# Softmax part between a product and its eviction, weight sums' DMAs on the GpSimd queue, tile pieces in twos, tail products two and then one

## The chip, the cores and the metric

The kernel runs on one core of a Trainium2 chip. The metric is the device time of one execution in microseconds (us). Before the change three runs gave 3805.22, 3813.81 and 3816.59; the median is 3813.81.

## The reference, cut to what matters

Two layers work on `x` of shape (2, 768, 64, 64), float32. Layer 0 is a Mamba block (input projection, 3x3 depthwise convolution, selective scan, layer norm, output projection). Layer 1 is an attention without keys; it and the end of layer 0 are what the change touches. `_gn` is a group norm over 32 groups.

```python
x = x + _L0_conv_ref(_gn(x), ...)
x = x + _L1_conv_ref(_gn(x), W_qkv, W_out, temp)

def _L1_conv_ref(x, W_qkv, W_out, temp):          # 12 heads of 64 channels, N = 4096 tokens
    w = (x3 @ W_qkv.T)                            # product 1, "p1": 768 x 768
    w_normed = w / max(norm over tokens, 1e-12)
    logits = sum over the head's channels of w_normed ** 2, times temp
    Pi = softmax(logits, over the heads)
    dots = sum over tokens of Pi / sum(Pi) * w ** 2
    out = -(w * Pi) / (1 + dots)
    return out @ W_out.T                          # product 3, "p3": 768 x 768
```

## The kernel before

All data are float32. Of each of the two images, layer 1 has 8 column tiles (`j`) of 512 tokens, and 768 channels are 6 chunks (`m` or `k`) of 128. A plain product of one (image, tile, chunk) is six 128x128 by 128x512 matmuls, which the profile counts as twelve instructions.

**Order.** The order of instructions is written by hand (`manual_schedule`); an engine runs its own in that order. What an engine's queue holds behind a waiting instruction waits too, and this is also so for SP, which issues most DMAs. Buffers of 512 columns are 46 slots, 79 from layer 1 on, in one list: `take` pops the oldest, `give` appends. Weights have 4 buffers (`wst`, `N_WEIGHT = 4`).

**Tail of layer 0.** `step(g)` runs one channel chunk through all stages of a pipeline. `scan(g)` (L512, L514) and `times_c(g)` (L521) are on VectorE. `out_proj(g)` (L574) is twelve steps behind and needs, every fourth step, `out_evict` (L586, VectorE) to free its two PSUM banks. When the input projections are used up, `step` does plain p1 products of image 0 in their place, one a step (`pq`, L663), evicted by ScalarE (L673, L674), all in the PSUM bank of `psA`. There are `N_TAIL` = 32 of them.

**Between.** Then `product` (`half_a`, `half_b`; tiles `mm`, L663 or L698) does the rest, with the banks `psA` and `psC` in turn. `half_a` loads weights up to four products ahead. Five products run beside the group norm of image 1, seven beside `weight_sums`, four more follow. `weight_sums` loads four quarter chunks of a weight matrix (L774), adds and subtracts them on GpSimd (L775 to L778) and stores four results to DRAM (`s_dr`, L782); loads and stores are issued by SP, the stores after the next product.

**Attention.** `attention(b)` goes over the 8 tiles: squares on ScalarE (L943), `head_rows` (L960), `head_columns` (L971), `softmax_a` (L977 to L980), `softmax_b` (L986 to L991 on VectorE, the transpose `pt` L995 on TensorE, its copy `pit` L999 on ScalarE), `spread` (L1011), `times_pi` (L1017) and `pi_sums` (L1024) on VectorE. One plain product is put into each tile as filler: its first half between `times_pi` and `softmax_a`, its second half before `softmax_b`. In `attention(0)` the filler is a p1 product, evicted on ScalarE; in `attention(1)` it is a p3 product, evicted on VectorE (L707) and stored by SP (L684).

**Block series.** The other products are done by `strassen`, which takes 7 half-size products for 8: a block is a (tile, `m`) with seven products of three 128x256 matmuls (L852). Series 1 has six p3 tiles of image 0 and six p1 tiles of image 1, series 2 the eight p3 tiles of image 1. Each tile needs twelve sums on GpSimd (`tile_sums`, L807), and before them six ScalarE operations: `scale_v` (L693) for p3, `norm_x1` (L651) for p1. `times` loads block weights up to seven halves ahead (L847). In a block ScalarE copies a product to `p5` (L906), VectorE adds it (L910), and the fifth product of the block waits for that. For p3, GpSimd adds `p5` too (L908). `copy` is L891, `evict` L875, L876 and L879, and the filling operations of the next tile come all at once at the start of a block.

Of the kernel before, what the change touches and what calls it, by code (L numbers as in the profile page):

```python
# [58 lines left out]

N_TAIL = BEHIND + 3 + AHEAD + 2  # L60

# [6 lines left out]
def both_layers(  # L68
# [621 lines left out]

    def scale_v(b, j):
        for k in range(KM):
            nc.scalar.activation(w1s[b, k, j], w1s[b, k, j], AF.Copy, scale=ats[b][:, k : k + 1])  # L693

    def p3_mm(d, w, po, ks):
# [41 lines left out]

    def half_b():
        p = cur["p"]
        kind, d = order[0][p]  # L740
        (p1_mm if kind == "p1" else p3_mm)(d, ready[p][0], cur["ps"], range(3, KM))
        if kind == "p1":
            p1_evict(d, cur["ps"])
            for t in cur["new"]:
                norm_x1(*t)
        else:
            p3_evict(d, cur["ps"], ready[p][1])
        ready[p] = None
# [20 lines left out]
    def weight_sums(kind, m):  # L769
        w = {"p1": qkvP, "p3": woutP}[kind]  # L770
        t = [take() for _ in range(6)]
        a11, a12, a21, a22, s1, s2 = [v[:, : KH * P].rearrange("p (k m) -> p k m", k=KH) for v in t]
        for v, (r, h) in zip((a11, a21, a22, a12), ((m, 0), (m + KH, 0), (m + KH, 1), (m, 1))):
            nc.sync.dma_start(v, w[r][:, h * KH : (h + 1) * KH, :])  # L774
        nc.gpsimd.tensor_add(s1, a21, a22)  # L775
        nc.gpsimd.tensor_sub(s2, s1, a11)
        nc.gpsimd.tensor_sub(a21, a11, a21)
        nc.gpsimd.tensor_sub(a12, a12, s2)  # L778

        def store():  # L780
            for q, v in enumerate((s1, s2, a21, a12)):
                nc.sync.dma_start(s_dr[kind][m, q], v)  # L782
            for v in t:
                give(v)

        return store

# [9 lines left out]
    def tile_sums(kind, b, j):  # L797
        x = [x1s[b, j, k] if kind == "p1" else w1s[b, k, j] for k in range(KM)]
        t = [take() for _ in range(5)]
        halves = [v[:, h] for v in t for h in (lo, hi)]  # L800
        b11, b12 = [[v[:, h] for v in x[:KH]] for h in (lo, hi)]
        b21, b22 = [[v[:, h] for v in x[KH:]] for h in (lo, hi)]
        t1, t3, t4 = [halves[KH * q : KH * (q + 1)] for q in range(3)]
        t2 = b12
        for o, p, q in ((t1, b12, b11), (t3, b22, b12), (t2, b22, t1), (t4, b21, t2)):
            for k in range(KH):
                nc.gpsimd.tensor_sub(o[k], p[k], q[k])  # L807
        tiles[kind, b, j] = {"b11": b11, "b21": b21, "b22": b22, "t1": t1, "t2": t2, "t3": t3, "t4": t4, "held": t}

    def tile_done(kind, b, j):  # L810
# [5 lines left out]

    def tile_prepare(kind, b, j, part):
        if part == 0:
            if kind == "p1":
                for k in range(KM):  # L820
                    load_x1(b, j, k)
            else:
                scale_v(b, j)
        elif kind == "p1" and part == 1:
            for k in range(KM):
                norm_x1(b, j, k)
        elif part == (2 if kind == "p1" else 1):
            tile_sums(kind, b, j)

    def strassen(todo, beside={}):  # L830

# [4 lines left out]
        seq = [v for v in seq if v[0] < len(blocks)]  # L836
        have, xr, at = {}, {}, {"load": 0, "use": 0}

        def times(dst, what, start=False):

            i = at["use"]
            while at["load"] < min(i + 7, len(seq)):
# [6 lines left out]
                at["load"] += 1  # L849
            full, half = have[i]  # L850
            for k in range(KH):
# [41 lines left out]

        load_res(0)
        y = first(0)
        x = copy(0, y)
        for q, (kind, b, j, m) in enumerate(blocks):
            load_res(q + 1)
            at_tile = q // KH
            if at_tile + 1 < len(todo):  # L900
                tile_prepare(*todo[at_tile + 1], q % KH)
            w = bank(psO, "po0", q)
            times(w[:, lo], "t1", start=True)
            times(x[:, lo], "b21")
            p5 = wk.tile([P, TL], F32, tag="sq", name=f"p5_{'_'.join(map(str, blocks[q]))}", bufs=3)[:, lo]
            nc.scalar.copy(p5, w[:, lo])  # L906
            if kind == "p3":
                nc.gpsimd.tensor_add(xr[q, 1][:, hi], p5, xr[q, 1][:, hi])  # L908
            times(y[:, lo], "t2")
            nc.vector.tensor_add(x[:, hi], y[:, lo], p5)  # L910
            y2 = first(q + 1) if q + 1 < len(blocks) else None
            evict(q, x[:, lo], 0, 0)
            times(y[:, lo], "t3")
            if kind == "p1":
                w1s[b, m + KH, j] = take()
                c22 = w1s[b, m + KH, j][:, hi]
                nc.vector.tensor_add(c22, y[:, lo], p5)
                nc.scalar.activation(
                    w[:, lo], c22, AF.Square, accum_out=ss[b][:, m + KH, 2 * j + 1 : 2 * j + 2]
                )  # L920
            else:
                evict(q, y[:, lo], 1, 1)
            times(x[:, hi], "b22")
            times(y[:, lo], "t4")
            if m == KH - 1:
                tile_done(kind, b, j)
            evict(q, x[:, hi], 0, 1)
            if kind == "p3":
                store_out(b, j, m, xr.pop((q, 0)))
            if y2 is not None:  # L930
                x = copy(q + 1, y2)
            evict(q, y[:, lo], 1, 0)
            if kind == "p3":
                store_out(b, j, m + KH, xr.pop((q, 1)))
            y = y2
            if q in beside:
                beside[q]()

# [88 lines left out]
    def attention(b, lead, more, behind):  # L1027
# [11 lines left out]
        for j in range(NQ):  # L1039
# [12 lines left out]
            pi_sums(b, j, range(2))  # L1052
            half_b()
            if not last:
                softmax_b(b, j + 1)
            times_pi(b, j, (4, 5))
# [19 lines left out]
        ats[b] = at  # L1076
        for part in range(3):
            tile_prepare(*behind, part)
        product(more)
# [7 lines left out]
    with tc.manual_schedule():  # L1087
# [23 lines left out]
        for v in range(N_EARLY[1]):  # L1111
            gn_piece(1, v)

        def step(g, prep=None):
            a, n = g + AHEAD, g + AHEAD + 2
# [3 lines left out]
            if n + 1 < NQ0:  # L1119

                for q in (n + 1, n + 2) if g < 0 else (n + 1,):
                    if q not in wis:
                        load_wi(q)
            elif NQ0 <= n + 1 < NQ0 + N_TAIL:
                wis[n + 1] = load_w1(qkvP[(n + 1) % KM])
            if BEHIND <= g + 1 < NQ0 + BEHIND:
# [11 lines left out]
            if n < NQ0:  # L1138
                in_proj(n)
            elif n < NQ0 + N_TAIL:  # L1140
                pas[n] = psA.tile([P, 512], F32, tag="psa", name=f"pq{n}")
                p1_mm(P1[n - NQ0][1], wis.pop(n), pas[n], range(KM))
            if g % 2 == 1 and 0 <= g - 5 < NQ0:
# [32 lines left out]
            if n < NQ0:  # L1176
# [13 lines left out]
            elif n < NQ0 + N_TAIL:  # L1190
                d = P1[n - NQ0][1]
                p1_evict(d, pas.pop(n))
                for k in {2: [0], 3: [1], 4: [2], 5: [3, 4, 5]}.get(d[2], []):
# [133 lines left out]
        for load, pe, dve in gn_next(1):  # L1327
# [3 lines left out]
            dve()  # L1331
        store = lambda: None
        for kind in ("p3", "p1"):
            for m in range(KH):
                product()
                store()
                store = weight_sums(kind, m)
        product()
        store()
        product(n1 - N_TAIL - 6 - 2 * KH)  # L1340
        todo = [("p3", 0, j) for j in range(NQ - N_FILL)] + [("p1", 1, j) for j in range(N_FILL, NQ)]
        attention(0, 1, 1, todo[0])
        beside = {3 * len(todo) - 6 + 2 * q: (lambda j: lambda: scale_v(0, j))(NQ - N_FILL + q) for q in range(N_FILL)}
        strassen(todo, beside)
        todo = [("p3", 1, j) for j in range(NQ)]
        attention(1, 1, 1, todo[0])
        strassen(todo)


# [133 lines left out]
```

## Time and profile before

| | |
|---|---|
| runs | 3805.22, 3813.81, 3816.59 us |
| profiled execution | 3809.74 us, its span 3808.0 us |
| busy in the span | PE 3571.5 (94%), DVE 2842.5 (75%), ACT 2562.5 (67%), POOL 1715.7 (45%) |
| matmul of the plain product | 12 instructions, 5.15 us where nothing holds them |
| matmul of the block product | 6 instructions, 1.29 us; 7 of them in 9.06 us a block |

PE is TensorE, PEld its weight loads, DVE VectorE, ACT ScalarE, POOL GpSimd, SP the queue that issues DMAs. Times in the text count from the start of the span. The stages, read from the timeline: layer 0 alone up to 2518; its last steps with the tail products up to 2886; products with group norm and weight sums up to 2988; `attention(0)` up to 3101; series 1 up to 3445; `attention(1)` up to 3583; series 2 to the end. A row of the timeline has start, duration, engine, line, operation, output<-input, shapes, count, and in brackets the engine's idle time before it with what ended it.

### The profile page before, as it was taken

Reading aid. Unit: us, or ns where it says so; the run is one execution under the profiler, and the core shown is the slowest. Engines: PE = TensorE matmul, PEld = TensorE weight load, DVE = VectorE, ACT = ScalarE, POOL = GpSimd, SP = SyncE. Lnnn points to the kernel's source line nnn. Section 1 sums busy time; section 2 is a strip of 40 time slices with the busy share of each in tenths; the row PEclk is TensorE's granted clock in tenths of the full one; section 3 lists DMA queues with packets and bytes.
Section 4 is the critical chain, followed back from the end, with each engine's and each line's share of the span. In section 5 each row is a group of like instructions: output and inputs, shape, how many; then the busy total and the mean of one; then the engine's idle time right before and its main releaser. Section 6 shows DMA issues by size and latency. Waiting matters only on the chain.

```text
span 3808.0 us, 36991 instructions
## 1 busy us (share of the span) xinstructions
PE 3571.5 (94%) x10882; PEld 1721.9 (45%) x10882; DVE 2842.5 (75%) x2554; ACT 2562.5 (67%) x4940; POOL 1715.7 (45%) x1713
## 2 busy tenths in 40 slices
PE   5877999999999999999999999999999999999899
PEld 3422333333333333333343333333344468884588
DVE  7699999999999999999999999997500342225422
ACT  2588888888888888888888888886523531343211
POOL 0255555565555555555555555654301023220142
PEclk9988999999999999999999999999999999999999
DMA  9677898998988989899898999976645348753487
GB/s 353 181 174 150 183 211 172 207 209 189 211 177 203 208 189 209 179 205 207 182 207 174 208 203 194 205 172 166 156 127 179 123 137 271 234 178 101 129 271 244
DMA packets 374921, 730.80 MB, mean 192 GB/s; under 512 B 43280, under 2 KB 111312, under 8 KB 370624
## 3 DMA queue, kind: packets, MB, share of 16 engines
q0 software_dynamic: 142560, 259.59, 40.8%
q1 hardware_dynamic: 232160, 468.85, 37.0%
q8 instruction: 88, 1.44, 0.2%
q14 instruction: 113, 0.93, 0.1%
HBM read 433.88 MB, written 60.03 MB: 130 GB/s over the span
## 4 chain that ended last, share of the span: by engine, by line
PE 41%; DVE 32%; DMA 8%; ACT 8%; issue 6%; POOL 3%; SPq 0%; DVEq 0%; POOLq 0%; ACTq 0%
DVE s L514 12%; PE po L574 7%; PE pa L352 7%; DVE acc L436 7%; PE po_p L852 6%; DVE s L512 5%; DVE da L521 5%; DMA u<-ysum 4%; PE psa_p L852 4%; PE acc_p L852 4%; PE mmp L663 3%; PE pq L663 3%; PE mmp L698 2%; POOL ysum L501 1%; ACT tm L402 1%
## 5 line engine op out<-in xcount | busy, mean ns | idle before, releaser
L352 PE MATMUL pa<-u,w 128*128 128x512 f32 (+1 forms) x2304 | 1048.7, 606 | 22.6 <-ACT carry L367 15.5
L574 PE MATMUL po<-u,w 128*128 128x512 f32 x2304 | 1036.7, 599 | 26.3 <-DVE u L586 26.3
L514 DVE TENSOR_TENSOR_SCAN s<-da,s 128x2052 f32<-128x2052 f32 x192 | 851.1, 4433 | 19.5 <-ACT u L307 0.5
L352 PEld LDWEIGHTS pa<-u,w 128*128 128x128 f32 x2304 | 434.4, 194 | 622.9 <-issue 492.0
L574 PEld LDWEIGHTS po<-u,w 128*128 128x128 f32 x2304 | 429.3, 190 | 619.2 <-issue 560.0
L501 POOL TENSOR_TENSOR ysum<-da 128x1024 f32<-128x1024 f32 x192 | 384.4, 2002 | 580.7 <-DVE da L521 455.4
L436 DVE SCALAR_TENSOR_TENSOR acc<-xs,pc,acc 128x512 f32<-128x512 f32 x741 | 558.3, 753 | 39.3 <-PE acc L422 12.9
L489 ACT ACTIVATE da<-dl,neg_a 128x512 f32<-128x512 f32 x768 | 489.7, 713 | 0.0
L512 DVE TENSOR_TENSOR s<-du,bc 128x2048 f32<-128x2048 f32 x192 | 438.9, 2286 | 57.8 <-POOL du L493 56.7
L408 POOL DMA_DIRECT2D tm<-tm x309 | 267.2, 865 | 447.0 <-ACT tm L402 408.1
L521 DVE TENSOR_TENSOR da<-s,bc 128x2048 f32<-128x2048 f32 x192 | 440.0, 2292 | 6.3
L508 POOL DMA_DIRECT2D u<-ysum x384 | 377.9, 1246 | 3.4 <-issue 2.4
L390 ACT ACTIVATE acc<-xs,pc 128x512 f32<-128x512 f32 x192 | 132.3, 689 | 282.8 <-DVE u L436 281.6
L402 ACT ACTIVATE tm<-xs,pc 128x512 f32<-128x512 f32 x486 | 317.1, 718 | 3.9 <-DMA tm<-tm 3.2
L493 POOL TENSOR_TENSOR du<-dl,u 128x512 f32<-128x512 f32 x192 | 243.5, 1268 | 0.0
L414 POOL DMA_DIRECT2D u<-tm x177 | 204.2, 1154 | 57.2 <-issue 41.2
L852 PE MATMUL po_p<-u,w 128*128 128x256 f32 x648 | 165.4, 384 | 0.0
L436 DVE SCALAR_TENSOR_TENSOR u<-xs,pc,acc 128x512 f32<-128x512 f32 x192 | 143.6, 748 | 9.5 <-DVE acc L436 0.4
L477 PE MATMUL pz<-xd,dt_w 48*128 48x512 f32 x384 | 113.1, 667 | 35.5 <-DVE gs_x L193 14.9
L505 ACT ACTIVATE u<-u,pc 128x512 f32<-128x512 f32 x192 | 137.0, 714 | 5.3 <-POOL du L493 5.2
L663 PE MATMUL pq<-u,w 128*128 128x512 f32 x300 | 135.2, 596 | 2.2 <-ACT pq L674 1.3
L443 ACT ACTIVATE u<-u,pc 128x512 f32<-128x512 f32 x192 | 124.4, 712 | 16.2 <-DMA u<-tm 15.7
(285 smaller groups left out, 4733.7 us busy)
## 6 DMA issues: line engine op xcount, KB each, us to landing
u<-ysum POOLq DMA_DIRECT2D x384, 256.0 KB, 5.6
tm<-tm POOLq DMA_DIRECT2D x309, 256.0 KB, 4.4
w<-in_wP SPq DMA_DIRECT2D x192, 384.0 KB, 4.6
w<-wo_dr SPq DMA_DIRECT2D x192, 384.0 KB, 4.9
u<-x SPq DMA_DIRECT2D x276, 256.0 KB, 5.2
w<-s_dr_p SPq DMA_DIRECT2D x240, 192.0 KB, 3.7
u<-tm POOLq DMA_DIRECT2D x177, 256.0 KB, 5.9
bc<-bc_dr SPq DMA_DIRECT2D x32, 1024.0 KB, 7.1
```

Of the source, the lines that this page charges most:

```text
L352: nc.tensor.matmul(pa[:, :nn], w[:, k, :], xts[i, k][:, :nn], start=(k == 0), stop=(k == KM - 1))
L402: nc.scalar.activation(tm.rearrange("p (h w) -> p h w", w=W), xs[:, dy : dy + TR, dx : dx + W], AF.Copy, scale=pc[:, c, PC_W + j : PC_W + ...
L436: nc.vector.scalar_tensor_tensor(dst, xs[:, dy : dy + TR, dx : dx + W], pc[:, c, PC_W + j : PC_W + j + 1], acc, ALU.mult, ALU.add)
L489: nc.scalar.activation(das[g % 2][:, n, 1:], deltas[g], AF.Exp, scale=neg_a[:, c, n : n + 1])
L501: nc.gpsimd.tensor_add(ysum[:, 0 : 2 + g % 2 : 1 + g % 2, :], da[:, 0:2, 1:], da[:, 2:4, 1:])
L508: nc.gpsimd.dma_start(us[g], ysums(g, n), accum_op=ALU.add)
L512: nc.vector.tensor_mul(s[:, :, 1:], dus.pop(g).unsqueeze(1).to_broadcast([P, NS, TL]), bc[:, :NS, :])
L514: nc.vector.tensor_tensor_scan(sf, das[g % 2].rearrange("p n l -> p (n l)"), sf, 0.0, ALU.mult, ALU.add)
L521: nc.vector.tensor_mul(das[g % 2][:, :, 1:], s[:, :, 1:], bc[:, NS:, :])
L574: nc.tensor.matmul(po[e], w[:, kk, e * P : (e + 1) * P], us[i * KI + k], start=(k == 0), stop=(k == KI - 1))
L663: nc.tensor.matmul(pa, w[:, k, :], x1s[b, j, k], start=(k == 0), stop=(k == KM - 1))
L852: nc.tensor.matmul(dst, half[:, k, :], tiles[blocks[seq[i][0]][:3]][what][k], start=(start and k == 0), stop=(k == KH - 1), skip_group_che ...
```

## The change

- Tail: 33 products, and step `NQ0 - 1` (the last with a scan) does two of them; from the sixth on, odd ones use the bank of `psC`.
- `weight_sums` issues its loads and stores on GpSimd's queue, stands before the product beside which it was, and stores at once.
- `half_b` takes a function that runs between its matmuls and its eviction; `attention` passes `softmax_b`.
- `strassen` is split: `prepare` (residual loads, the first six half weights, the first tile's scaling and sums) is called in `attention` before its last product; `products` does the rest.
- The ScalarE and GpSimd operations for the next tile are queued as single jobs and issued in twos at three places of a block (GpSimd's in fours in the third block of a tile). The two p3 tiles left for `attention(1)` are scaled in this way in the last tile of series 1.

```diff
-N_TAIL = BEHIND + 3 + AHEAD + 2
+N_TAIL = BEHIND + 3 + AHEAD + 2 + 1
...
-    def half_b():
+    def half_b(between=lambda: None):
...
         (p1_mm if kind == "p1" else p3_mm)(d, ready[p][0], cur["ps"], range(3, KM))
+        between()
         if kind == "p1":
             p1_evict(d, cur["ps"])
...
         for v, (r, h) in zip((a11, a21, a22, a12), ((m, 0), (m + KH, 0), (m + KH, 1), (m, 1))):
-            nc.sync.dma_start(v, w[r][:, h * KH : (h + 1) * KH, :])
+            nc.gpsimd.dma_start(v, w[r][:, h * KH : (h + 1) * KH, :])
...
-        def store():
-            for q, v in enumerate((s1, s2, a21, a12)):
-                nc.sync.dma_start(s_dr[kind][m, q], v)
-            for v in t:
-                give(v)
-        return store
+        for q, v in enumerate((s1, s2, a21, a12)):
+            nc.gpsimd.dma_start(s_dr[kind][m, q], v)
+        for v in t:
+            give(v)
...
+        def prepare():
+            load_res(0)
+            load(6)
+            run(tile_scalar(*todo[0]))
+            run(tile_sums(*todo[0]))
...
+        def jobs_of(q):
+            at_tile, part = divmod(q, KH)
+            if at_tile + 1 == len(todo):
+                if part == 0:
+                    scalar_jobs.extend(last)
+                return
+            kind, b, j = todo[at_tile + 1]
+            if kind == "p1" and part == 0:
+                for k in range(KM):
+                    load_x1(b, j, k)
+            if part == (1 if kind == "p1" else 0):
+                scalar_jobs.extend(tile_scalar(kind, b, j))
+            if part == (2 if kind == "p1" else 1):
+                pool_jobs.extend(tile_sums(kind, b, j))
+
+        def some_jobs(q):
+            run(scalar_jobs, 2)
+            run(pool_jobs, 4 if q % KH == 2 else 2)
...
                 nc.scalar.copy(p5, w[:, lo])
                 if kind == "p3":
                     nc.gpsimd.tensor_add(xr[q, 1][:, hi], p5, xr[q, 1][:, hi])
+                some_jobs(q)
                 times(y[:, lo], "t2")
                 nc.vector.tensor_add(x[:, hi], y[:, lo], p5)
                 y2 = first(q + 1) if q + 1 < len(blocks) else None
                 evict(q, x[:, lo], 0, 0)
+                some_jobs(q)
                 times(y[:, lo], "t3")
...
                 if y2 is not None:
                     x = copy(q + 1, y2)
+                some_jobs(q)
                 evict(q, y[:, lo], 1, 0)
...
-            half_b()
-            if not last:
-                softmax_b(b, j + 1)
+            half_b(lambda: last or softmax_b(b, j + 1))
...
-        for part in range(3):
-            tile_prepare(*behind, part)
+        behind()
         product(more)
...
+        def tail(g):
+            q = g + AHEAD + 2 - NQ0
+            return [v for v in ([q] if g < NQ0 - 1 else [q, q + 1] if g == NQ0 - 1 else [q + 1]) if 0 <= v < N_TAIL]
...
-            elif n < NQ0 + N_TAIL:
-                pas[n] = psA.tile([P, 512], F32, tag="psa", name=f"pq{n}")
-                p1_mm(P1[n - NQ0][1], wis.pop(n), pas[n], range(KM))
+            for q in tail(g):
+                bank, tag = (psC, "acc") if q > 3 and q % 2 else (psA, "psa")
+                pas[NQ0 + q] = bank.tile([P, 512], F32, tag=tag, name=f"pq{q}")
+                p1_mm(P1[q][1], wis.pop(NQ0 + q), pas[NQ0 + q], range(KM))
...
             for m in range(KH):
+                weight_sums(kind, m)
                 product()
-                store()
-                store = weight_sums(kind, m)
-        product()
-        store()
-        product(n1 - N_TAIL - 6 - 2 * KH)
+        product(n1 - N_TAIL - 5 - 2 * KH)
```

More of the change, by code (lines that the diff above doesn't have):

```diff
@@ L689, in p3_load @@
         return load_w1(woutP[d[2]]), xr
-    def scale_v(b, j):
-        for k in range(KM):
-            nc.scalar.activation(w1s[b, k, j], w1s[b, k, j], AF.Copy, scale=ats[b][:, k : k + 1])
     def p3_mm(d, w, po, ks):
@@ L804, in tile_sums @@
         t2 = b12
-        for o, p, q in ((t1, b12, b11), (t3, b22, b12), (t2, b22, t1), (t4, b21, t2)):
-            for k in range(KH):
-                nc.gpsimd.tensor_sub(o[k], p[k], q[k])
+        jobs = [
+            (lambda o, p, q: lambda: nc.gpsimd.tensor_sub(o, p, q))(o[k], p[k], q[k])
+            for o, p, q in ((t1, b12, b11), (t3, b22, b12), (t2, b22, t1), (t4, b21, t2)) for k in range(KH)
+        ]
         tiles[kind, b, j] = {"b11": b11, "b21": b21, "b22": b22, "t1": t1, "t2": t2, "t3": t3, "t4": t4, "held": t}
+        return jobs
     def tile_done(kind, b, j):
@@ L814, in tile_done, with tile_scalar, piece, run @@
             give(t)
-    def tile_prepare(kind, b, j, part):
-        if part == 0:
+    def tile_scalar(kind, b, j):
+        def piece(k):
             if kind == "p1":
-                for k in range(KM):
-                    load_x1(b, j, k)
-            else:
[L823 to L830, printed above, removed]
+                norm_x1(b, j, k)
+            else:
+                nc.scalar.activation(w1s[b, k, j], w1s[b, k, j], AF.Copy, scale=ats[b][:, k : k + 1])
+        return [(lambda k: lambda: piece(k))(k) for k in range(KM)]
+    def run(jobs, n=None):
+        for _ in range(len(jobs) if n is None else min(n, len(jobs))):
+            jobs.pop(0)()
+    def strassen(todo, last=()):
         blocks = [t + (m,) for t in todo for m in range(KH)]
@@ L837, in strassen, with load @@
         have, xr, at = {}, {}, {"load": 0, "use": 0}
-        def times(dst, what, start=False):
-            i = at["use"]
-            while at["load"] < min(i + 7, len(seq)):
+        scalar_jobs, pool_jobs = [], []
+        def load(until):
+            while at["load"] < min(until, len(seq)):
                 q, w = seq[at["load"]]
@@ L849, in times @@
                 at["load"] += 1
+        def times(dst, what, start=False):
+            i = at["use"]
+            load(i + 7)
             full, half = have[i]
@@ L892, in copy @@
             return x
[L894 to L937, printed above, removed]
@@ new lines, in some_jobs, with products @@
+        def some_jobs(q):
+            run(scalar_jobs, 2)
+            run(pool_jobs, 4 if q % KH == 2 else 2)
+        def products():
+            y = first(0)
+            x = copy(0, y)
+            for q, (kind, b, j, m) in enumerate(blocks):
+                load_res(q + 1)
+                jobs_of(q)
+                w = bank(psO, "po0", q)
+                times(w[:, lo], "t1", start=True)
+                times(x[:, lo], "b21")
+                p5 = wk.tile([P, TL], F32, tag="sq", name=f"p5_{'_'.join(map(str, blocks[q]))}", bufs=3)[:, lo]
+                nc.scalar.copy(p5, w[:, lo])
+                if kind == "p3":
+                    nc.gpsimd.tensor_add(xr[q, 1][:, hi], p5, xr[q, 1][:, hi])
+                some_jobs(q)
+                times(y[:, lo], "t2")
+                nc.vector.tensor_add(x[:, hi], y[:, lo], p5)
+                y2 = first(q + 1) if q + 1 < len(blocks) else None
+                evict(q, x[:, lo], 0, 0)
+                some_jobs(q)
+                times(y[:, lo], "t3")
+                if kind == "p1":
+                    w1s[b, m + KH, j] = take()
+                    c22 = w1s[b, m + KH, j][:, hi]
+                    nc.vector.tensor_add(c22, y[:, lo], p5)
+                    nc.scalar.activation(
+                        w[:, lo], c22, AF.Square, accum_out=ss[b][:, m + KH, 2 * j + 1 : 2 * j + 2]
+                    )
+                else:
+                    evict(q, y[:, lo], 1, 1)
+                times(x[:, hi], "b22")
+                times(y[:, lo], "t4")
+                if m == KH - 1:
+                    tile_done(kind, b, j)
+                evict(q, x[:, hi], 0, 1)
+                if kind == "p3":
+                    store_out(b, j, m, xr.pop((q, 0)))
+                if y2 is not None:
+                    x = copy(q + 1, y2)
+                some_jobs(q)
+                evict(q, y[:, lo], 1, 0)
+                if kind == "p3":
+                    store_out(b, j, m + KH, xr.pop((q, 1)))
+                y = y2
+            run(scalar_jobs)
@@ L940, in squares @@
+        return prepare, products
     def squares(b, j):
@@ L1123, in step @@
                         load_wi(q)
-            elif NQ0 <= n + 1 < NQ0 + N_TAIL:
-                wis[n + 1] = load_w1(qkvP[(n + 1) % KM])
+            for q in tail(g + 1)[: int(g != NQ0 - 1)]:
+                wis[NQ0 + q] = load_w1(qkvP[q % KM])
             if BEHIND <= g + 1 < NQ0 + BEHIND:
@@ L1139, in step @@
                 in_proj(n)
-            elif n < NQ0 + N_TAIL:
-                pas[n] = psA.tile([P, 512], F32, tag="psa", name=f"pq{n}")
-                p1_mm(P1[n - NQ0][1], wis.pop(n), pas[n], range(KM))
+            for q in tail(g):
+                bank, tag = (psC, "acc") if q > 3 and q % 2 else (psA, "psa")
+                pas[NQ0 + q] = bank.tile([P, 512], F32, tag=tag, name=f"pq{q}")
+                p1_mm(P1[q][1], wis.pop(NQ0 + q), pas[NQ0 + q], range(KM))
+            for q in tail(g + 1)[int(g != NQ0 - 1) :]:
+                wis[NQ0 + q] = load_w1(qkvP[q % KM])
             if g % 2 == 1 and 0 <= g - 5 < NQ0:
@@ L1189, in step @@
                         norm_x1(0, 0, k)
-            elif n < NQ0 + N_TAIL:
-                d = P1[n - NQ0][1]
-                p1_evict(d, pas.pop(n))
+            for q in tail(g):
+                d = P1[q][1]
+                p1_evict(d, pas.pop(NQ0 + q))
+                if d[1] == (N_TAIL - 1) // KM:
+                    continue
                 for k in {2: [0], 3: [1], 4: [2], 5: [3, 4, 5]}.get(d[2], []):
@@ L1331, in both_layers @@
             dve()
-        store = lambda: None
         for kind in ("p3", "p1"):
             for m in range(KH):
+                weight_sums(kind, m)
                 product()
-                store()
-                store = weight_sums(kind, m)
-        product()
-        store()
-        product(n1 - N_TAIL - 6 - 2 * KH)
[L1341 to L1347, printed above, removed]
+        product(n1 - N_TAIL - 5 - 2 * KH)
+        rest = range(NQ - N_FILL, NQ)
+        scaled = []
+        prepare, products = strassen([("p3", 0, j) for j in range(NQ - N_FILL)] + [("p1", 1, j) for j in range(N_FILL, NQ)], scaled)
+        attention(0, 1, 1, prepare)
+        for j in rest:
+            scaled += tile_scalar("p3", 0, j)
+        products()
+        prepare, products = strassen([("p3", 1, j) for j in range(NQ)])
+        attention(1, 1, 1, prepare)
+        products()
 @with_exitstack
```

## The prediction

> **What bounds the kernel now.** First the page: busy shares and slices.
>
> ```profile
> PE 3571.5 (94%) x10882; PEld 1721.9 (45%) x10882; DVE 2842.5 (75%) x2554; ACT 2562.5 (67%) x4940; POOL 1715.7 (45%) x1713
> PE   5877999999999999999999999999999999999899
> DVE  7699999999999999999999999997500342225422
> ```
>
> Up to slice 27 VectorE and TensorE are both full; from about 2640 us on only TensorE is, and all that the change touches lies there. So an edit is worth what it takes from TensorE's idle time after 2640. The second view is the list of TensorE's waits from 2560 on (who, for whom, us in total, times, longest):
>
> ```profile
> PE pt L995 <- DVE pi L990: 17.1, 9, 3.8
> PE po L574 <- DVE u L586: 9.0, 3, 5.1
> PE acc_p L852 <- DVE po_p L910: 7.5, 6, 4.5
> PE psa_p L852 <- DMA w<-woutP: 7.3, 1, 7.3
> PE mmp L663 <- ACT v L651: 6.0, 1, 6.0
> PE pq L663 <- ACT pq L674: 3.8, 3, 1.3
> PE psa_p L852 <- DVE po_p L910: 1.6, 2, 0.8
> ```
>
> Six places, of which the change addresses each. The third view, the timeline of TensorE, shows what a wait costs beyond itself:
>
> ```profile
> 2740.39 7.88 PE L574 MATMUL po<-u,w 128*128 128x512 f32 x12 [5.09 <-DVE u L586]
> 2952.67 2.07 PE L663 MATMUL mmp<-v,w 128*128 128x512 f32 x2 [6.01 <-ACT v L651]
> 2954.54 3.97 PE L663 MATMUL mmp<-u,w 128*128 128x512 f32 x6
> 2960.92 2.74 PE L663 MATMUL mmp<-u,w 128*128 128x512 f32 x6
> 3486.64 1.16 PE L995 MATMUL pt<-ident,pi 128*128 128x128 f32 x8 [1.65 <-DVE pi L990]
> 3582.92 1.19 PE L852 MATMUL psa_p<-v,w 128*128 128x256 f32 x2 [7.30 <-DMA w<-woutP]
> ```
>
> After idle times over about 3 us matmuls run at half speed for a while (twelve take 7.88 us instead of 5.31; six 3.97 instead of 2.74). I count this with each wait.
>
> **The change part by part**, all times in the profiled execution (3809.7 us).
>
> *Tail 2-1.* At 2740.39 `po` waits for L586, which stands in VectorE's queue behind the last scan (L514 at 2732.97, L521 at 2737.44). That chain takes nothing from the tail products, so the release stays. TensorE ended its tail product at 2735.1; with one product more (5.15 us) it arrives at 2740.25. Idle 5.1 and slow clock 7.88 - 5.31 = 2.6 go: 7.7 us, since the moved product disappears later. Cover: the fourth tile's last x pieces, now wanted at 2735; ScalarE evicts the second product at about 2728.8 to 2730.2 and norms four pieces (2.9 us for four at 2871.94) by about 2733.5. If that is late, up to 5.1 comes back. SP's loads of weights stay within four buffers; each is issued when a product or `out_proj` frees one.
>
> *Two banks in the tail.* The last two of the waits for L674 (1.27 each) go. But the first product after the tail waits for weights (1.85 us), which SP issues behind two stores of sums (L608) that follow the last-but-one eviction on ScalarE. This eviction moves forward by 1.4, not 2.5, relative to the last `out_proj`. Gain 1.4 (0 to 2.5).
>
> *Weight sums on GpSimd's queue.* At 2952.67 TensorE waits for a norm (L651) of a piece that SP loaded only at 2946.60, behind stores waiting for GpSimd's sums:
>
> ```profile
> 2940.85 3.31 SPq L782 DMA_DIRECT2D s_dr_p<-v  x4
> 2946.60 0.43 SPq L648 DMA_DIRECT2D v<-x  x1
> ```
>
> With these on GpSimd, SP never waits for sums. Gone are 6.0, the slow clock 1.05 + 1.23 = 2.3, and 0.7 at 2977.26, where ScalarE was late from another such piece: 9.0. New on GpSimd: 8 DMA issues a set, bounded by its own DMA rows (0.87 at L408 to 1.25 at L508), 4 sums of 0.99, a load's landing between 2.6 (SP's weight quarters) and 5.8 (L594): 13.5 to 20 us a set, I take 15, nearer the plain rows. Queued behind a waiting GpSimd instruction are only the next sets. GpSimd is idle from 2867.6, and the slots that the first sets take were returned many steps before, so six sets run to about 2958. About 33 slots are free in the list at the first set, and set and product take 8; a slot of set k comes round four sets later, when it has been stored. The series read `s_dr` at 3098. Cost 0.
>
> The Trainium skill, "DMA: Bandwidth & Descriptors", section "Issuing engines are not separate DMA queues", speaks against this part: transfers of all issuing engines share the same DMA engines, and another issuer only saves the sequencer's time to issue. By that rule alone this part is worth nothing and the sum is 9.0 smaller. The rows above show more than issue time, namely SP's waiting for GpSimd (L782), which the rule doesn't speak of.
>
> *First weights of a series.* Series 2 begins with 7.3 idle; its weights were issued at 3577.78, behind the store of the last filler product (3576.37), landing 5.0 later. Now they follow the store before, at 3571.00: issue at 3572.4, landing 3577.4, and TensorE is ready at 3575.45. 2.0 stays, 5.3 goes, and the slow start (1.19 + 1.91 + 3.74 against 0.59 + 1.03 + 2.32) gives 2.9: 8.2 (5 to 10). Series 1 had no wait, but gets one: with 27 instead of 28 products in the first list, the last now uses `psA`, which the series' first block also takes. Its eviction stood behind six scalings and ended at 3102.04, where the block began at 3100.65: -1.4.
>
> *Pieces in twos.* `p5` (L906) stood behind six norms or, at 3393.75 to 3401.65, six scalings and six norms; L910 came late. Waits of four times 0.79, 4.46 and 0.23 go, and a slow stretch after 3402.52 (1.22 + 1.91 + 2.61 against 0.59 + 1.03 + 1.46, 2.7): 10.5. Two norms (1.5 us) fit ScalarE's idle times at the three places, 3.2, 1.6 and about 0.4, the last with 2.3 of slack between the next L906 and L910. GpSimd's sums end a block before they are read. The waits of the last blocks (0.59 and 0.58) stay, and so do 2.63 and 2.41 for weights behind x loads at 3248 and 3278, which keep their place.
>
> *Softmax part before the eviction.* In `attention(1)` `pt` waits 1.65 because L707, which waits for the product, stands before L986 to L990:
>
> ```profile
> 3485.03 0.69 DVE L707 TENSOR_TENSOR u<-mmp,u 128x512 f32<-128x512 f32 x1 [2.16 <-PE mmp L698]
> 3486.32 0.26 DVE L990 COPY pi<-e 128x192 f32<-128x192 f32 x1
> 3034.43 0.26 DVE L990 COPY pi<-e 128x192 f32<-128x192 f32 x1
> 3035.78 1.05 PE L995 MATMUL pt<-ident,pi 128*128 128x128 f32 x8
> ```
>
> The last two rows are `attention(0)`, where no eviction is in VectorE's way: `pi` is ready 1.1 before TensorE needs it, and a tile takes 11.20 us (3035.78 to 3046.98) against 13.11 (3486.64 to 3499.75). Seven times 1.91 is 13.4. VectorE now waits 1.2 at L707 with `times_pi` and `pi_sums` behind it; put into the 11.20, it reaches the next tile's `times_pi` 0.6 late, which the 1.08 that it waits for L971 takes up. Bound: 0 to 13.4. After the last tile the slow clock (3.78 for four and 1.91 for two at 3555.78, against 1.88 and 1.02) should go: 2.8.
>
> Sum: 7.7 + 1.4 + 9.0 + 8.2 - 1.4 + 10.5 + 13.4 + 2.8 = 51.6. The profiled execution would take 3758.1. It is 4 below the median of the three runs; the mean of all four is 3811.3, so I predict 3759.7, rounded to 3760.
>
> **The rivals.** *A: a wait takes the place.* The x pieces or series weights stay late, because their DMAs meet GpSimd's traffic: 9.0 and half of 8.2 fail, 3773. For it: a weight landed within 3.0 to 5.1 us in that stretch. Against: 33 free slots of buffer.
>
> *B: VectorE becomes the bound of `attention(1)`*: slack is only 0.5 us a tile by the count above. Then the 13.4 and 2.8 shrink to nothing: 3776. Against: 9 us of VectorE work in a tile of 11.20.
>
> *C: slower.* The sets run one after another on GpSimd, and the squares of `attention(0)` (at about 2972 in the new run) take slots of set 5. With a set of T us from 2867.6, these are free at 2870 + 5T: from T = 20.5 TensorE waits, and from T = 33 (63 us lost against 51.6 won) the kernel is over 0.3% slower; at 34 it is 3828. The rows give at most 20.
>
> *D: nothing.* The waits come back elsewhere for 40 us or more: 3805.
>
> **How the numbers follow.** 0.3% is 11 us, about what a measurement of this kernel can tell from no change. My forecast (3748 to 3772) has 0.66, A 0.12, B 0.11, C 0.07, D 0.04. Faster: 0.66 + 0.12 + 0.11 = 0.89; same 0.04; slower 0.07. The range: from 3748 less 2 for a series 2 whose weights land in time, up to A and B together (3789); it leaves out C, D and little more.
>
> **What would show it.** Right: no wait of `po` near 2740; one tile of `attention(1)` in 11.2; no idle SP behind L782; L807 and L651 in twos between L906 and L891; a wait of about 2 for weights at the start of series 2 and of 1.4 for L674 at series 1. Wrong: `pt` still waiting for L990, squares or norms waiting for a DMA out of L782, or a set on GpSimd over 20 us.

## The result and the profile after

| | before | after |
|---|---|---|
| runs, median | 3813.17 us (4 runs, 3805.22 to 3816.59) | 3762.81 us (4 runs, 3758.20 to 3765.68) |
| profiled execution, its span | 3809.74, 3808.0 us | 3758.20, 3756.3 us |

The ratio is 0.987 (95% interval 0.985 to 0.9889): faster, by 50 us in the medians and 51.7 in the spans of the profiled executions. Line numbers are those of each run's own kernel, so `pt` is L995 before and L1022 after. First the page after, busy shares and slices:

```profile
PE 3558.0 (95%) x10882; PEld 1719.9 (46%) x10882; DVE 2842.8 (76%) x2554; ACT 2562.5 (68%) x4940; POOL 1742.7 (46%) x1761
...
PE   5877999999999999999999999999999999999999
```

The 8 among the last twelve slices of before is gone. TensorE's waits from 2560 on (for whom, us in total, times, longest):

```profile
PE pt L1022 <- DVE pi L1017: 5.6, 2, 3.8
PE po L574 <- DVE u L586: 4.9, 2, 4.1
PE mmp L663 <- DMA w<-qkvP: 4.8, 1, 4.8
PE acc_p L852 <- DMA w<-woutP: 2.6, 1, 2.6
...
PE psa_p L852 <- ACT mmp L674: 1.3, 1, 1.3
```

`pt` waited 17.1 before and 5.6 now, the waits for `po_p` (9.1) and the 7.3 for the first weights of series 2 are nearly gone. The wait for the weights of the first product after the tail has grown from 1.8 to 4.8. The timeline of TensorE at these places:

```profile
2732.79 5.31 PE L663 MATMUL pq<-u,w 128*128 128x512 f32 x12
2738.07 5.42 PE L574 MATMUL po<-u,w 128*128 128x512 f32 x12
...
2860.73 15.61 PE L663 MATMUL pq<-v,w 128*128 128x512 f32 x36
2881.17 8.13 PE L663 MATMUL mmp<-v,w 128*128 128x512 f32 x12 [4.83 <-DMA w<-qkvP]
...
3445.47 1.05 PE L1022 MATMUL pt<-ident,pi 128*128 128x128 f32 x8
3456.67 1.05 PE L1022 MATMUL pt<-ident,pi 128*128 128x128 f32 x8
...
3533.58 1.53 PE L852 MATMUL psa_p<-u,w 128*128 128x256 f32 x6 [0.41 <-DMA w<-woutP]
```

`po` starts right behind the product put ahead of it, with no bracket and at full speed (12 in 5.42). The last three tail products are one row of 36 without a wait between them. Then comes the longer wait, and 8.13 for twelve, where the same product took 5.39 before:

```profile
2886.05 5.39 PE L663 MATMUL mmp<-v,w 128*128 128x512 f32 x12 [1.85 <-DMA w<-qkvP]
```

The granted clock of TensorE is 0.50 from 2881 to 2885 in the trace of after and 1.00 from 2889 on. A tile of `attention(1)` takes 3456.67 - 3445.47 = 11.20.

Where the 51.7 of the spans are, from the starts of the same instructions in both traces:

| stretch (in the trace of after) | predicted | measured |
|---|---|---|
| layer 0 up to its last scan | 0 | 2.3 |
| up to the last `out_proj`, with the 5.15 of the product put ahead | 7.7 | 7.6 |
| up to `attention(0)`, less these 5.15 (two banks 1.4, weight sums 9.0) | 10.4 | 6.8 |
| `attention(0)`, with the wait for L674 at series 1 | -1.4 | -1.6 |
| series 1 (pieces in twos) | 10.5 | 11.2 |
| `attention(1)`, up to `pp` | 16.2 | 16.2 |
| first weights of series 2, up to the end | 8.2 | 9.2 |

The 2.3 of layer 0 are scatter: in the eleven kernels, after and ten of those below, that have the same instructions up to there, the last scan began at 2730.65 to 2735.68. Before, at 2732.97, lies inside this range, and after, at 2730.65, is its earliest. Below, "net" means: the difference of the spans less the difference at the last scan.

### The profile page after: what moved, and what is told of

Read it like the earlier page. It is cut to its first block, busy times and chain, and to the rows that moved or that the text cites. A ratio compares the mean times of both kernels' runs of the same rounds, so it can differ in the third digit from the quotient of the medians.

```text
span 3756.3 us, 36987 instructions
## 1 busy us (share of the span) xinstructions
PE 3558.0 (95%) x10882; PEld 1719.9 (46%) x10882; DVE 2842.8 (76%) x2554; ACT 2562.5 (68%) x4940; POOL 1742.7 (46%) x1761
## 4 chain that ended last, share of the span: by engine, by line
PE 39%; DVE 37%; ACT 10%; DMA 6%; issue 6%; POOL 2%; SPq 0%; DVEq 0%; POOLq 0%; ACTq 0%
DVE s L514 14%; DVE acc L436 8%; PE po_p L852 6%; PE po L574 6%; DVE da L521 6%; DVE s L512 5%; PE pa L352 5%; PE psa_p L852 4%; PE acc_p L852 4%; PE mmp L663 4%; DMA u<-ysum 3%; PE pq L663 3%; PE mmp L694 2%; ACT tm L402 1%; ACT da L489 1%
## 5 line engine op out<-in xcount | busy, mean ns | idle before, releaser
L408 POOL DMA_DIRECT2D tm<-tm x309 | 268.0, 867 | 447.1 <-ACT tm L402 385.1
L508 POOL DMA_DIRECT2D u<-ysum x384 | 378.8, 1250 | 3.7 <-issue 2.6
```

The lines of the kernel that those rows point to most:

```text
L508: nc.gpsimd.dma_start(us[g], ysums(g, n), accum_op=ALU.add)
```

## The experiments

Each is the changed kernel with one edit, profiled and timed. The ratio is to the kernel before on the same chip.

**Undo the softmax order** (u_soft).

```diff
-            half_b(lambda: last or softmax_b(b, j + 1))
+            half_b()
+            if not last:
+                softmax_b(b, j + 1)
```

> The changed kernel with the softmax part issued after the eviction again (all else kept). Theory (each gain is TensorE idle time and slow clock taken away at its own place, and the terms add): a tile of attention(1) goes from 11.20 back to 13.11 us, seven times 1.9 = 13.3, and the slow clock after the last tile returns (2.9): the span is 16 us longer than the changed kernel's 3756.35, about 3772.5, with nothing moved ahead of 3434. Rival (the tiles became faster because work came to them earlier from the other parts, the order in VectorE's queue matters little): under 5 us longer, no wait of pt for pi over 1 us.

3779.15 us, ratio 0.992 (0.9905 to 0.9935). The stretch from the first tile of `attention(1)` to `pp` is 16.15 longer, from the start of series 2 on nothing more is lost: 15.5 net at the end. A row of the timeline, tile by tile:

```profile
3466.39 1.16 PE L1022 MATMUL pt<-ident,pi 128*128 128x128 f32 x8 [1.64 <-DVE pi L1017]
```

The wait of 1.65 of before is back, seven times. The rival falls: without this order the other edits bring nothing of this part. That 16.15 meets the 16.2 of the table so closely is luck: 1.6 of it are a slow stretch at the first tile, which neither before nor after has (see u_tail), and after the last tile only 1.3 of the predicted 2.8 came back; the seven tiles by themselves are 13.3, where 13.4 was predicted.

**Undo the weight sums' queue** (u_sums): `nc.gpsimd.dma_start` becomes `nc.sync.dma_start` in both places, and the order of issue is again that of before.

> The changed kernel with the loads and stores of weight_sums on SP's queue again, the stores issued a product later as before (all else kept). Theory (SP stood still behind stores that waited for GpSimd's sums, so the pieces of x came late): the wait of a product for ScalarE's norm (about 6) and the slow clock behind it return: +9.4, span about 3765.7. Rival (another issuing engine saves only issue time on SP): no such wait, within 1.5 us of 3756.35. Second question: the first product after the tail now waits 4.83 for its weights, which land 5.6 after their issue while GpSimd's first set stores and its second loads; if these transfers share what the weights need, the landing goes back to about 4.1 here and the wait to about 3.4.

3771.62 us, ratio 0.9899 (0.9884 to 0.9913). From the first product to `attention(0)` it takes 11.1 longer, 11.4 net at the end; counted from the last `out_proj`, as in the table, it is 9.3, since the first product's weights come 1.8 earlier here. Two rows of the timeline of TensorE, and rows of SP:

```profile
2943.95 1.13 PE L663 MATMUL mmp<-v,w 128*128 128x512 f32 x2 [3.76 <-ACT v L651]
...
2963.41 2.93 PE L663 MATMUL mmp<-u,w 128*128 128x512 f32 x3 [2.89 <-ACT mmp L674]
```

```profile
2928.72 0.43 SPq L648 DMA_DIRECT2D u<-x  x1
2932.68 1.39 SPq L779 DMA_DIRECT2D s_dr_p<-u  x2
...
2938.72 0.33 SPq L648 DMA_DIRECT2D v<-x  x1
2942.14 1.39 SPq L779 DMA_DIRECT2D s_dr_p<-u  x2
```

SP stands for 2.6 to 3.4 us in front of the stores of each set but one (L779 here), so x pieces go out every 8 to 10 us, where TensorE uses one every 5.15. The wait is the predicted one. The rule of the Trainium skill that the prediction weighed ("DMA: Bandwidth & Descriptors", section "Issuing engines are not separate DMA queues": another issuer only saves time to issue), by which, as the prediction put it, this part is worth nothing, does not cover it. An estimate from SP's rows: eight DMAs at 0.47 (L771, four in 1.88), a weight and a piece are 4.6 us to issue, less than the 5.15 of a product; it is the waiting that makes 8 to 10 of it.

**Undo only the stores' queue** (sums_stores): the stores on SP a product later as before, the loads on GpSimd.

> The changed kernel with only the stores of weight_sums back on SP's queue, issued a product later as before; the loads stay on GpSimd's queue. Theory (SP's standing still behind stores that wait for GpSimd's sums is what made the x pieces late): nearly the whole +11.1 of the run with both on SP comes back from the first product to attention(0), waits for L651 or L674 included. Rival (a DMA issued elsewhere saves its issue time on SP, 0.43 us each): loads and stores are 24 and 24, so about half, +5 to 6.

3761.07 us, ratio 0.9868 (0.9854 to 0.9881): nothing is lost. Both theories miss. From the first product to `attention(0)` it even takes 1.3 less than after; that product itself waited 7.2 for its weights, not 4.8, so that from the last `out_proj` it is 1.1 more, and 2.1 net at the end, 1.6 of these at the first tile of `attention(1)` (see u_tail). With the loads on GpSimd its sums run ahead of SP, and the stores find them ready:

```profile
2922.78 0.43 SPq L648 DMA_DIRECT2D u<-x  x1
2923.31 0.85 SPq L779 DMA_DIRECT2D s_dr_p<-u  x2
2924.26 1.15 SPq L779 DMA_DIRECT2D s_dr_p<-v  x2
```

So the stores' queue doesn't count once the loads are elsewhere, and the half that the rival gave to 24 issues isn't there. What the rows of u_sums show is a ring: SP issued a set's loads, had to stand in front of its stores until the sums were done, and only then issued the loads of the next. Taking the loads out breaks it.

**Undo the pieces in twos** (u_pieces, then u_pieces2).

```diff
             if part == (2 if kind == "p1" else 1):
                 pool_jobs.extend(tile_sums(kind, b, j))
+            run(scalar_jobs)
+            run(pool_jobs)
```

> The changed kernel with all scalings, norms and sums of a tile issued at once at the head of the block in which their first pair is issued now (the place of the kernel before; all else kept). Theory (p5's copy stood behind six or twelve of them on ScalarE): series 1 gets 11.2 us longer (333.26 to about 344.5), series 2 by under 1, span about 3767.5, with waits of acc_p or psa_p for po_p of 4 to 5 us back. Rival (what helped series 1 was its weights being there from the start): series 1 within 2 us of 333.3.

3764.99 us, ratio 0.9883 (0.9869 to 0.9898). Series 1 is 6.4 longer (from the start of its first matmul to the start of its last), between theory and rival: five waits for `po_p` of 0.79, weights landing 1.1 later in all with 1.4 of slower matmuls behind them, but no wait of 4 or 5. In this kernel the twelve scalings for the filler products stay in the last tile, in twos, where no norms are. So the second version also puts these back where they were:

```diff
             if at_tile + 1 == len(todo):
-                if part == 0:
-                    scalar_jobs.extend(last)
                 return
...
-            run(scalar_jobs)
+                if last and q in (len(blocks) - 6, len(blocks) - 4):
+                    run(last, KM)
```

> The changed kernel with the pieces at once as in the earlier run of that kind (+6.4 in series 1), and the twelve scalings for the fill products also as in the kernel before: six at the end of a block, twice, so that the first six stand right ahead of the six norms of the next tile on ScalarE. Theory (the rest of the 11.2 comes from this one stack of twelve): one wait of acc_p or psa_p for po_p of about 4.5 with a slow stretch behind it, series 1 about 344.5 us long, 11.2 more than the changed kernel. Rival (the rest came from the landing of weights): 339.7 again, no wait over 0.8 for po_p.

3776.52 us, ratio 0.9909 (0.9895 to 0.9922); series 1 takes 344.69 instead of 333.26, 11.4 more. The queue of ScalarE there, and TensorE:

```profile
3384.32 0.71 ACT L817 ACTIVATE v<-v,at 128x512 f32<-128x512 f32 x1
3384.93 0.71 ACT L817 ACTIVATE u<-u,at 128x512 f32<-128x512 f32 x1
3385.54 2.55 ACT L817 ACTIVATE v<-v,at 128x512 f32<-128x512 f32 x4
3387.99 0.80 ACT L651 ACTIVATE v<-v,bias,scale 128x512 f32<-128x512 f32 x1
3388.70 1.51 ACT L651 ACTIVATE u<-u,bias,scale 128x512 f32<-128x512 f32 x2
3390.11 2.21 ACT L651 ACTIVATE v<-v,bias,scale 128x512 f32<-128x512 f32 x3
3392.22 0.35 ACT L929 COPY p_p<-po_p 128x256 f32<-128x256 f32 x1
```

```profile
3393.09 1.22 PE L852 MATMUL acc_p<-u,w 128*128 128x256 f32 x2 [4.46 <-DVE po_p L934]
```

`p5` (L929) stands behind six scalings and six norms, and TensorE waits 4.46. The two versions differ by 5.0, and the stack of twelve is worth more than that, since 2.5 of the first version's 6.4 are the late weights, of which this one has 0.5.

**Undo the early first weights** (u_first): `load_res(0)` from `prepare` to `products`, and `load(6)` taken out.

> The changed kernel with the first weights and residuals of a block series loaded when its products begin and no longer in prepare (all else kept). Theory: series 2 starts with a wait of about 7.3 us for its weights and slow matmuls behind it: +9.6, span about 3766; series 1 unchanged. Rival (weights landed in 3.6 us instead of 5.0 because less other traffic was there, and the earlier issue was worth only the 5.3 of its 5.3 us): +5 to 6.

3771.92 us, ratio 0.9903 (0.9886 to 0.992). The start of series 2 is 6.6 later and the slow matmuls behind it cost 2.4 more: 9.0.

```profile
3542.94 1.19 PE L852 MATMUL psa_p<-v,w 128*128 128x256 f32 x2 [6.99 <-DMA w<-woutP]
```

**Undo the tail** (u_tail).

```diff
-N_TAIL = BEHIND + 3 + AHEAD + 2 + 1
+N_TAIL = BEHIND + 3 + AHEAD + 2
...
-            return [v for v in ([q] if g < NQ0 - 1 else [q, q + 1] if g == NQ0 - 1 else [q + 1]) if 0 <= v < N_TAIL]
+            return [v for v in [q] if 0 <= v < N_TAIL]
```

> The changed kernel with one tail product a step and 32 of them instead of 33 (two banks and all else kept). Theory (po waits for VectorE's scan whatever TensorE does; a product put ahead fills that wait): po near 2740 waits 5.1 again and runs at half speed behind it, +7.6; the first list has 28 products again, so its last one leaves the bank that the series uses first, and the wait of 1.3 for L674 at the start of series 1 goes: +6.3 in all, span about 3762.7 if layer 0 takes as long (the runs so far differ there by up to 4 us with the same code). Rival (the early product only moved the wait on to the first weights after the tail): +1 to 2.

3767.18 us, ratio 0.9886 (0.9872 to 0.9899); 11.2 net, 5 more than the theory's 6.3.

```profile
2738.17 7.18 PE L574 MATMUL po<-u,w 128*128 128x512 f32 x10 [5.10 <-DVE u L586]
```

At its place it is as expected: from the last scan to the last `out_proj` 2.6 more with a product less in it, 2.6 + 5.15 = 7.8. The wait for L674 at series 1 went (1.3). What came on top lies elsewhere: the first product waited 6.3 for its weights instead of 4.8, weights of series 1 landed later (1.6), and a slow stretch at the first tile of `attention(1)` cost 1.6. The same 1.6 stood in eight of the twelve runs told here, whatever their edit, and neither in before nor in after: `pt` waits 1.80 there in all of them, but from 3443 to 3448 in u_bank the granted clock is 0.66, and from 3434 to 3438 in after, the same place, 1.00. I take it for scatter, which was not tested by repeating.

**One bank in the tail** (u_bank): `psA` for all `pq`.

> The changed kernel with all tail products in one bank (all else kept). Theory (the prediction's term): two waits of 1.27 for the eviction return, and the first product's weights are issued 1 to 1.5 us later behind it, so that its wait shrinks by only part: from last po to the first product after the tail +1 to +1.4, span about 3757.6 less the difference in layer 0. Rival (read from the marks: from before to after this stretch lost 2.6): two banks bring TensorE to the weights earlier and so into a longer idle time and slow clock, and with one bank the stretch is 2.6 shorter, span about 3753.8. If theory holds, the 2.6 came from the landing of the weights beside GpSimd's transfers, not from the banks.

3767.11 us, ratio 0.9883 (0.987 to 0.9897); 11.1 net. Both theories miss. From the last `out_proj` to the first product it is 3.8 longer (2.7 up to `attention(0)`), and the step with two products, where I expected nothing, costs 4.2 (2.4 of waiting, 1.8 of slower matmuls). TensorE and ScalarE there:

```profile
2717.26 5.31 PE L663 MATMUL pq<-u,w 128*128 128x512 f32 x12
2725.00 7.11 PE L663 MATMUL pq<-u,w 128*128 128x512 f32 x12 [2.43 <-ACT pq L674]
```

```profile
2723.67 0.20 ACT L518 COPY s<-state 128x4 f32<-128x4 f32 x1 [3.69 <-DVE s L514]
2723.77 0.58 ACT L673 COPY u<-pq 128x512 f32<-128x512 f32 x1
```

The eviction of the first of the two products stands on ScalarE behind L518, which waits for a scan. With one bank the second product waits for that. So the second bank also carries the tail's 2-1, a dependence that the prediction didn't see.

**Delay the sets of weight sums** (sums_late).

```diff
+        kind, d = order[0][cur["p"]]
+        product()
+        nc.gpsimd.tensor_copy(gate, w1s[d[0], d[2], d[1]][:, :4])
         for kind in ("p3", "p1"):
...
-        product(n1 - N_TAIL - 5 - 2 * KH)
+        product(n1 - N_TAIL - 6 - 2 * KH)
```

> The changed kernel with one small copy on GpSimd ahead of the first set of weight sums, which reads the output of the first product after the tail; so GpSimd's transfers start only after that product's eviction. Theory (the weights of that product land late because GpSimd's first set moves data at the same time): they land 3.8 to 4.2 us after their issue (5.2 to 6.9 with the sets beside them, 3.8 with the sets on SP), the wait is 3.0 to 3.4 instead of 4.8, and the span 1.5 to 2 us shorter; six sets still end before series 1 needs them. Rival (landing is chance): 5 us or more again, no gain.

3780.71 us, ratio 0.9919 (0.9904 to 0.9933). The first weights landed 3.6 after their issue and the wait was 2.87, as the theory says; the twelve matmuls behind it still take 7.05, the first three of them 2.90. First sums_late, then the issue in after, whose product starts 5.6 later, at 2881.17:

```profile
2876.47 1.82 SPq L657 DMA_DIRECT2D w<-qkvP  x4
2880.10 2.90 PE L663 MATMUL mmp<-v,w 128*128 128x512 f32 x3 [2.87 <-DMA w<-qkvP]
```

```profile
2875.59 2.59 SPq L657 DMA_DIRECT2D w<-qkvP  x4
```

Over the kernels that issue these weights at this place: issue to start 5.1 to 7.9 us in the eight with GpSimd's sets beside it, 3.6 to 4.2 in the three without (before, u_sums and this one). But the kernel became 18 slower, for another reason:

```profile
2998.77 2.08 PE L1022 MATMUL pt<-ident,pi 128*128 128x128 f32 x8 [18.91 <-DVE pi L1017]
```

```profile
2976.39 0.58 ACT L673 COPY v<-mmp 128x512 f32<-128x512 f32 x1 [4.79 <-POOL u L774]
...
2981.82 0.63 ACT L970 ACTIVATE v<-u 128x512 f32<-128x512 f32 x1 [3.08 <-DMA s_dr_p<-v]
```

Evictions and squares on ScalarE take slots of the fifth and sixth set, which are stored only up to 2990, and the first softmax stands behind them. This is the prediction's rival C with its mechanism, brought about by a later start instead of a longer set.

**A better version, in three steps** (better, better2, better3).

```diff
+            if g == NQ0 + BEHIND + 2:
+                for q in range(2):
+                    ready[q] = (load_w1(qkvP[order[0][q][1][2]]),)
...
-        bank, tag = ((psA, "psa"), (psC, "acc"))[p % 2]
+        bank, tag = ((psA, "psa"), (psC, "acc"))[(len(order[0]) - p) % 2]
```

> The changed kernel with two edits: the weights of the first two products after the tail are loaded in the last step ahead of the stores of sums, and the products' banks are counted from the end of their list, so that its last one leaves psA to the series. Theory: the wait of 4.8 for weights and the slow clock behind it (2.7) go, and the 1.3 to 1.4 for L674 at series 1: -8.9, span about 3747.5 (plus up to 4 for layer 0's scatter). Rival (the products then run into the pieces of x, which are loaded behind the same stores): a wait for L651 of 2 to 5 in one of the first six products, span about 3751.

3757.33 us, ratio 0.9854 (0.9841 to 0.9868); 3.2 net in place of 8.9, and its five runs (3750.29 to 3759.59) still overlap with those of after. The wait of 4.8 and the one at series 1 are gone, but the rival was right in kind: two products later TensorE waits for another load behind the same stores, a constant of the group norm (`gsel_in`, 1.58) and slow matmuls behind it, and the weights of series 1 came later.

```diff
-                for k in range(KM):
-                    load_x1(b, j, k)
+                load_jobs.extend((lambda k: lambda: load_x1(b, j, k))(k) for k in range(KM))
...
+            run(load_jobs, 2)
             run(scalar_jobs, 2)
```

> The kernel of the run before with one edit more: in series 1 the six pieces of x of the next tile are loaded in twos and no longer six in a row ahead of weights. Theory (weights stand behind six loads on SP's queue at two places): the waits of 2.6 and 1.5 for w go, another -4.1. Rival (they wait for something else, the landing): within 1 us of the run before.

3752.25 us, ratio 0.9848 (0.9834 to 0.9861). Series 1 takes 328.45, 6.1 less than in better (334.55), where 4.1 were expected: of the two waits for weights behind x loads only one of 1.2 is left. At the end the gain is 5.3 net, since 1.6 are lost to the slow stretch at the first tile of `attention(1)`.

```diff
+        sets = [(kind, m) for kind in ("p3", "p1") for m in range(KH)]
...
             step(g)
+            if g - NQ0 in (4, 5, 6, 8, 9, 10):
+                weight_sums(*sets.pop(0))
...
-        for kind in ("p3", "p1"):
-            for m in range(KH):
-                weight_sums(kind, m)
-                product()
-        product(n1 - N_TAIL - 5 - 2 * KH)
+        product(n1 - N_TAIL - 5)
```

> The kernel better2 with the six sets of weight sums issued earlier, one after each of six steps of layer 0's tail (steps NQ0+4, 5, 6, 8, 9, 10), and none behind the tail. Theory (from 2878 to 2895 SP's burst of stores, weights and pieces of x and GpSimd's sets fill the DMA engines, so that weights land 7.0 and gsel_in about 9 after their issue; between 2780 and 2860 they move only 133 GB/s): with the sets gone from there the wait of pb_y for gsel_in (1.4) and the slow clock behind it (2 to 3) go, -3.4, span about 3746.7 (layer 0's scatter apart), and the DMA share of 2878 to 2895 falls well below 9 tenths. Rival 1 (SP's burst fills them alone): landing and wait stay, no gain. Rival 2 (sets in the tail keep GpSimd from the residuals): po or the first weights late, +2 to 5.

3748.04 us, ratio 0.9838 (0.9824 to 0.9852); 3.9 net beyond better2, 3.4 were expected. All five runs (3743.03 to 3753.47) lie below all four of after. The DMA view of 2875 to 2895 (40 slices of 0.5 us in tenths busy; issues with KB each and median us to landing), first of better2, then of better3:

```profile
DMA  0000755899999799999999999999999998999979
...
w<-qkvP SPq DMA_DIRECT2D x4, 384.0 KB, 7.0
```

```profile
DMA  0920996799999998989499951100067999400000
...
w<-qkvP SPq DMA_DIRECT2D x4, 384.0 KB, 3.6
```

With GpSimd's sets beside SP's burst the DMA engines are busy from 2877 to the end of the window, and a weight takes 7.0 to land; without them the burst is over by 2887, and it takes 3.6. `pb_y` no longer waits:

```profile
2888.73 1.50 PE L198 MATMUL pb_y<-gs_y,u 32*128 32x1 f32 x12
```

GpSimd's residuals in the tail were not disturbed: TensorE waits 5.1 in all for `po` (4.9 in after).

## Why the prediction was right

3760 was predicted and 3762.81 measured. Its reasoning, that each edit is worth the idle time and slow clock of TensorE at its own place, holds in the undo runs at these places: 7.8 for the tail (7.7 predicted), 9.3 for the weight sums (9.0), 11.4 for the pieces (10.5), 9.0 for the first weights (8.2), 14.5 for the softmax order without the slow stretch at its first tile (13.4 + 2.8). The signs of rival B stayed away: VectorE reaches the next tile in time, with 0.65 to spare in front of L1004.

```profile
3464.24 0.21 DVE L1004 TENSOR_REDUCE mx<-pl 128x4 f32<-128x48 f32 x1 [0.65 <-PE pl L998]
```

That the total was met to a tenth, 51.6 in the sum and 51.7 in the spans, is luck in part. Of the 51.7, 2.3 are layer 0's scatter; with 0.7 more at the pieces and 1.0 more at series 2 they make up for 3.6 that were lost at the two banks and the weight sums. The profiled execution is also the fastest of its four, and free of the slow stretch of 1.6 at the first tile of `attention(1)`. At the end of the span the terms do not simply add: undone one by one, the six parts cost 70.9 net together (with u_pieces2 for the pieces), the whole change gained 49.4. The tail and the two banks need each other, and five of the six runs have the slow stretch.

Four terms were off.

- *Two banks*: +1.4 was predicted, and the stretch with the weight sums brought 6.8 instead of 10.4. Undoing each edit singly cost 9.3 and 2.7 there, so neither is worth less than predicted when the rest is in place. The loss lies at the first product after the tail: by the prediction's count its wait would have been about 3.0 (1.27 + 1.27 + 1.85 - 1.4), and it was 4.8, with 2.7 of slow clock behind it. The step left the landing of the weights as it was in the trace of before (4.15 from issue to start) although another part put GpSimd's transfers next to them; it measured 5.6, and 3.6 with these delayed. And it let a wait of 3 stand without the slow clock that the prediction counts with its other waits; sums_late has it (7.05 for twelve) behind 2.87. Rival A had named the traffic, but for the x pieces and the series' weights, where it didn't occur. The two banks also carry the tail's 2-1 (4.2), which the prediction put down to the extra product alone.
- *First weights*: the wait of 2.0 that was to stay measured 0.4, since the weights landed in 3.6 instead of 5.0.
- *A set on GpSimd*: 15 us were taken, 12 to 14 measured (first loads at 2862.5, last store at 2939). The issue was priced by L408 and L508 (0.87 to 1.25), which are accumulating DMAs; a plain one took GpSimd 0.54 us. So the sets ended 18 us earlier than counted, 5 of these because they began earlier. This lay beside other work; sums_late shows what stands behind that cover.
- *Slow clock*: "after idle times over about 3 us" is not borne out as a limit. In u_bank twelve matmuls take 7.11 behind a wait of 2.43, and in better six block matmuls take 1.59 behind one of 3.13, against 1.46 at full speed. The waits with which the sum counted it did have it.

The mechanism given for the weight sums was right, but not complete: SP's standing in front of the stores was one half of a ring, and taking the loads out was enough (sums_stores); the stores alone were not tried on GpSimd.

## What to carry to other kernels

When a queue issues both the loads and the stores of another engine's work, look for the ring: here it was enough to issue the loads elsewhere. A landing time from a trace holds for the traffic of that trace; when an edit moves transfers, look which transfers then run beside those that somebody waits for, and move bulk work to where the DMA slices are low. And when two edits meet at one place (two products a step, two banks), ask of each what it is worth without the other.

## What the hardware showed beyond expectation

- A 384 KB weight landed 3.6 us (median) after its issue in the window 2875 to 2895 of better3, without GpSimd's sets, and 7.0 in that of better2, with them, at 302 GB/s over all engines there.
- A plain DMA issue took GpSimd 0.54 us, accumulating ones 0.88 (L594), 0.87 (L408) and 1.25 (L508).
- Matmuls at half speed don't follow from the length of the wait alone. Behind the same wait of 1.80 for `pt` at the first tile of `attention(1)` eight matmuls took 1.16 in after and 2.00 in u_bank. What else decides is not shown here.
- The granted clock of the spans was 0.98 in all profiled executions, and still the same layer 0 took up to 5 us more or less, more than three of the eight terms of the sum; only marks taken net of it tell these apart.
